# A matrix-square-root layer and a Fourier layer on 32x32 images: m and y side by side in one tile, the inverse transform's end in two matmuls, layer 0's statistics for two images at once, one scale for m and its transpose, and shorter roots

## The chip, the cores and the metric

The kernel runs on one core of one Trainium2 chip. The metric is the device time of one execution in microseconds (us); lower is better. The time before is the median of three runs.

## The reference

The input x holds 32 images of 32 channels of 128 x 128 numbers in fp32. Two layers follow each other, and each adds something to its input.

```
def _gn(v, G=16, eps=1e-5):          # mean and variance over 2 channels x 128 x 128
    return (g - m) / sqrt(s + eps)

def _L0_conv_ref(A):                 # for each of the 32*32 matrices of 128 x 128
    normA = sqrt(sum(A*A));  Y = A / normA;  Z = I
    for _ in range(5):
        T = 0.5 * (3*I - Z @ Y);  Y = Y @ T;  Z = T @ Z
    return Y * sqrt(normA)

def _L1_conv_ref(x, weights1, weights2):
    x_dht = fftn(x, axes=(2, 3)).real
    top = einsum('bixy,ioxy->boxy', x_dht[:, :, :32, :32], weights1)
    bot = einsum('bixy,ioxy->boxy', x_dht[:, :, -32:, :32], weights2)
    return ifftn(zeros with top and bot set in).real

x = x + _L0_conv_ref(_gn(x))
x = x + _L1_conv_ref(_gn(x), L1_conv_weights1, L1_conv_weights2)
```

Layer 0 is by far the larger part: 1024 matrices, each with a chain of products of 128 x 128 matrices.

## The kernel before

**Groups.** Four channels of one image make a group, so there are 256 groups. A group's four matrices are one tile of 128 partitions x 512 columns, and each PSUM bank holds one group's product. `products` (L304 to L308) is four TensorE matmuls, one for each matrix, into one bank; `transposed` (L310 to L314) is four TensorE transposes.

**The iteration.** The five steps of the reference are folded into two polynomials of fourth degree and a last linear one, in `newton` (L400) and `quartic` (L364). `quartic` forms v from the product mb m and from m (L367), then w, which is v transposed plus r, and q from the product v w plus a multiple of the identity (L394). After the first quartic ScalarE copies the product q m, scaled, out of PSUM as y (L404), then q y as m (L406), then m transposed as mb (L408). After the second quartic TensorE makes q m and q y, each as four matmuls with a 128-column moving operand and with q as the stationary one (L412). ScalarE writes the first as w in one instruction of 512 columns (L413) and the second as y, in four instructions of 128 columns, each with its own channel's scale (L416). VectorE turns the product w q into t (L418) and adds the product t y to the input, kept in xt (L420). Between such steps stands `yield from rest`, which is two yields.

**Near and far groups.** A "near" group's v is transposed by TensorE. A "far" group's v (images 1 to 18) is transposed in blocks by VectorE (L373), written to DRAM and read back in another order (L375, L383 or L386), and GpSimd adds r to it (L388), so TensorE has no transpose to do there.

**Order of the work.** A Python loop at the end writes all instructions out. It has nine lanes, each with one group under way, and goes round them; in each round a lane does one step of its group. A new group starts every 3 rounds (far) or 5 rounds (near). Side work is threaded in at fixed lanes of a round: the layer-0 statistics (`prep`), layer 1's forward transform (`settle`, `forward`, `summed`, `spectrum`), the products with the weights, and the inverse transform. Instructions inside `kept` stay in the order in which they were written on their queue; a planner may place the others differently. Every engine then works through its own queue in order.

**Layer 0's statistics.** `prep(b)` (L187) handles one image. It loads the image's transposed copy a second time, as eight tiles of 4 channels (L194, on ScalarE's DMA queue), and takes VectorE's `bn_stats` of each channel, 128 elements a partition (L202). `moments` (L162) sums means over the partitions with a matmul by a constant matrix (L172); a second such matmul sums the squares (L213). Then come some twenty small VectorE instructions, and two square roots by `root` (L150): ScalarE's Sqrt and one Newton step on VectorE in four instructions. The results are the scales and offsets with which `staged` (L333) normalizes a group: GpSimd writes m from xt (L348) and ScalarE writes mb, the matrix that is not transposed, in place (L359). Each has its own scale: sc and offm for m, scr and off for mb.

**Layer 1's statistics.** `summed` (L479) takes per-channel sums. One matmul with a stationary operand of 128 columns (q repeated four times over the columns, `b_qr`, L487) leaves the variance on all partitions (L492), and a second one with 32 columns gives the means (L495). `root` and a reciprocal give the inverse deviation (L502 to L504).

**The inverse transform.** `inverse` (L826) works on one image. Its end, for each half e of the channels, is three sets of four matmuls (L877). The four of a set use 32 rows of the array each and run side by side. The first set gives the cosine part (64 columns of each of four channels), the second the sine part (63 columns each), and the third one column of each channel, 4 in all, which goes to the place before the sine columns. ScalarE copies the second half of the columns out (L889), VectorE adds the first half to the image (L894).

**Room.** Tiles come from pools with a fixed number of buffers for each name (`rooms`, L259): y and m have four each, and two more while the pool for the early part stands. At the end `weights` (L743) loads the last group's weights into tiles of the layer-0 pools that are no longer needed, in the order of a list of names.

Of the kernel before, what the change touches and what calls it, by code (L numbers as in the profile page):

```python
# [48 lines left out]
EYE = 36 / 16  # L49
QS = EYE / QD  # L50
MS = -QA * QS
# [17 lines left out]
def conv_preact_kernel(  # L69
# [3 lines left out]
    xt_in: bass.AP,  # L73
    wk: bass.AP,
# [75 lines left out]
    def root(v, n, tag, f=1.0):  # L150

        s0 = small.tile([P, n], F32, tag=f"{tag}_s0", name=f"{tag}_s0")
        nc.scalar.activation(s0, v, AF.Sqrt, scale=1.0 / (f * f))
        q = small.tile([P, n], F32, tag=f"{tag}_q", name=f"{tag}_q")
        nc.vector.reciprocal(q, s0)
        nc.vector.tensor_mul(q, q, v)
        nc.vector.scalar_tensor_tensor(q, q, 1.0 / (f * f), s0, ALU.mult, ALU.add)
        s = small.tile([P, n], F32, tag=f"{tag}_s", name=f"{tag}_s", bufs=3)
        nc.vector.tensor_scalar_mul(s, q, 0.5 * f)
        return s  # L160

    def moments(st, tag):  # L162

        per = st.shape[1] // G
        f = st.rearrange("p (g c) (e t) -> p g (c e) t", c=per, t=3)
        ms = small.tile([P, G], F32, tag=f"{tag}_ms", name=f"{tag}_ms")
        nc.vector.tensor_reduce(ms, f[:, :, :, 1], AX.X, ALU.add)
        yield from pause  # L170
        pm = bank()[:, 0, 0:G]
        nc.tensor.matmul(pm, avg_mean, ms, start=True, stop=True)  # L172
        nm = small.tile([P, G], F32, tag=f"{tag}_nm", name=f"{tag}_nm", bufs=2)
        nc.vector.tensor_scalar_mul(nm, pm, 2 / per)
        d = small.tile([P, G, 2 * per], F32, tag=f"{tag}_d", name=f"{tag}_d")
        nc.vector.tensor_tensor(
            d, f[:, :, :, 1], nm[:, :, None].to_broadcast([P, G, 2 * per]), ALU.add
        )
        nc.vector.tensor_mul(d, d, d)
        nc.vector.scalar_tensor_tensor(d, d, 128.0 / per, f[:, :, :, 2], ALU.mult, ALU.add)  # L180
        return ms, nm, d
# [5 lines left out]
    def prep(b, made):  # L187

        st = small.tile([P, C, 6], F32, tag="a_st", name=f"a_st{b}", bufs=2)
        tiles = []  # L190

        def load(i):
            t = stp.tile([P, 4, P], F32, tag="xs", name=f"xs{b}_{i}")
            kept(nc.scalar.dma_start(out=t, in_=xt_in[b, :, 4 * i : 4 * i + 4, :]))  # L194
            tiles.append(t)

        for i in range(3):
            load(i)
        yield
        for i in range(C // 4):  # L200
            for c in range(4):
                nc.vector.bn_stats(st[:, 4 * i + c, :], tiles[i][:, c, :])  # L202
            yield
            if i + 3 < C // 4:
                load(i + 3)
        _, nm, d = yield from moments(st, "a")
        q = small.tile([P, C], F32, tag="a_qs", name=f"a_qs{b}")
        nc.vector.tensor_reduce(
            q, d.rearrange("p g (c e) -> p (g c) e", e=2), AX.X, ALU.add
        )  # L210
        yield from pause
        pq = bank()[:, 0, 0:C]
        nc.tensor.matmul(pq, avg_mean, q, start=True, stop=True)  # L213

        v = small.tile([P, C + G], F32, tag="a_v", name=f"a_v{b}")
        nc.vector.tensor_scalar_mul(v[:, 0:C], pq, -512 / (P * P))
        yield
        vg = small.tile([P, G], F32, tag="a_vg", name=f"a_vg{b}")
        nc.vector.tensor_reduce(
            vg, v[:, 0:C].rearrange("p (g c) -> p g c", c=2), AX.X, ALU.add  # L220
        )
        nc.vector.tensor_scalar(v[:, C:], vg, 0.5, EPS, ALU.mult, ALU.add)
        s = root(v, C + G, "a_r")
        iv = small.tile([P, C + G], F32, tag="a_inv", name=f"a_inv{b}")
        nc.vector.reciprocal(iv, s)
        yield

        sc = small.tile([P, C], F32, tag="a_sc", name=f"a_sc{b}", bufs=2)
        nc.vector.tensor_scalar_mul(sc, iv[:, 0:C], MS / P)
        n = small.tile([P, G, 2], F32, tag="a_n", name=f"a_n{b}")  # L230
        nc.vector.tensor_tensor(  # L231
            n,
            s[:, 0:C].rearrange("p (g c) -> p g c", c=2),
            iv[:, C:, None].to_broadcast([P, G, 2]),
            ALU.mult,
        )
        nn = small.tile([P, C], F32, tag="a_nn", name=f"a_nn{b}")
        nc.vector.tensor_scalar_mul(
            nn, n.rearrange("p g c -> p (g c)"), P * (1.5 / EYE) ** 2
        )  # L240
        sn = root(nn, C, "a_t")

        scr = small.tile([P, C], F32, tag="a_scr", name=f"a_scr{b}", bufs=2)
        nc.vector.tensor_scalar_mul(scr, sc, QR * QS / MS)
        off = small.tile([P, G, 2], F32, tag="a_off", name=f"a_off{b}", bufs=2)
        nc.vector.tensor_tensor(
            off,
            scr.rearrange("p (g c) -> p g c", c=2),
            nm[:, :, None].to_broadcast([P, G, 2]),
            ALU.mult,  # L250
        )
        off = off.rearrange("p g c -> p (g c)")
        offm = small.tile([P, C], F32, tag="a_offm", name=f"a_offm{b}", bufs=2)
        nc.vector.tensor_scalar_mul(offm, off, MS / (QR * QS))
        made[b] = (nm, sc, offm, sn, scr, off)
        yield


    rooms = dict(b=(4, 2), xt=(10, 4), x=(3, 2), r=(5, 2), v=(3, 3), w=(3, 2), q=(4, 2), y=(4, 2))  # L259
    rooms.update(m=(4, 2), mb=(2, 1), t=(3, 2), y4=(2, 2), turn=(0, 4))  # L260
    turns = dict.fromkeys(rooms, 0)

    def four(tag, more):
        n, m = rooms[tag]
        if more:
            turns[tag] += 1
            if turns[tag] % (n + m) >= n:
                return early.tile([P, 4, P], F32, tag=tag + "_early", name=tag, bufs=m)
        return sets.tile([P, 4, P], F32, tag=tag, name=tag, bufs=n)
# [63 lines left out]
    def staged(b, g, nm, sc, offm, sn, scr, off):  # L333
# [10 lines left out]
        for j in range(4):  # L344
# [12 lines left out]
            else:  # L357
                on_scalar(m[:, j, :], xt[:, j, :], offm, sc, c)
            on_scalar(mb[:, j, :], mb[:, j, :], off, scr, c)  # L359
# [4 lines left out]
    def quartic(m, mb, r, far, more, wide):  # L364


        v = plus(products(mb, m), -1 / (QA * QR * QS), m, "v", more)  # L367
# [26 lines left out]
        q = plus(products(v, w), 1 / (16 * QS * QS), eye, "q", more)  # L394
# [5 lines left out]
    def newton(g, sn, xt, m, mb, r, far, more):  # L400
# [3 lines left out]
        y = taken(products(q, m), "y", more, 1 / MS)  # L404
        yield from rest
        m = taken(products(q, y), "m", more, MS)  # L406
        yield from rest
        mb = taken(transposed(m), "mb", more, QR * QS / MS)  # L408
# [3 lines left out]
        pw, py = products(q, m), products(q, y)  # L412
        w, y = taken(pw, "t", more, 1 / MS), four("y4", more)  # L413
        for j in range(4):
            c = 4 * g + j
            nc.scalar.mul(y[:, j, :], py[:, j, :], sn[:, c : c + 1])  # L416
        yield from rest
        t = plus(products(w, q), -0.5 * EYE / 1.5, eye, "t", more)  # L418
# [60 lines left out]
    def summed(b, st):  # L479

        ms, _, d = yield from moments(st, "b")
        yield

        q = small.tile([P, G], F32, tag="b_qs", name=f"b_qs{b}")
        nc.vector.tensor_reduce(q, d, AX.X, ALU.add)
        qr = small.tile([P, 4, G, 2], F32, tag="b_qr", name=f"b_qr{b}")
        nc.vector.tensor_copy(qr, q[:, None, :, None].to_broadcast([P, 4, G, 2]))  # L487
        mr = small.tile([P, G, 2], F32, tag="b_mr", name=f"b_mr{b}")
        nc.vector.tensor_copy(mr, ms[:, :, None].to_broadcast([P, G, 2]))
        yield from pause  # L490
        pv = bank()[:, 0, :]
        nc.tensor.matmul(  # L492
            pv[:, 0:1], qr.rearrange("p l g c -> p (l g c)"), avg_v, start=True, stop=True
        )
        nc.tensor.matmul(  # L495
            pv[0:C, 1:2], mr.rearrange("p g c -> p (g c)"), avg_0, start=True, stop=True
        )
# [4 lines left out]
        s = root(v[:, 0:1], 1, "b_r", 256.0)  # L502
        r = small.tile([P, 1], F32, tag="b_inv", name=f"b_inv{b}")
        nc.vector.reciprocal(r, s)  # L504
# [238 lines left out]
    def weights():  # L743


        kinds = [("b", 2)] * 3 + [("x", 2), ("b", 4), ("x", 4), ("x", 10), ("y", 10), ("y", 10)]
        kinds += [("m", 11)] * 2 + [("r", 12)] * 4 + [("mb", 15)] * 2 + [("v", 15)] * 2
        kinds += [("w", 16)] * 2 + [("y", 16), ("m", 16), ("r", 17)] + [("q", 19)] * 3
        first = B * C // 4 - 10
        for half in range(4, 2 * KK):  # L750
            while True:
                if kinds and kinds[0][1] <= len(steps_of_last):
                    kind = kinds.pop(0)[0]
                    break
                if len(settled) > first and settled[first] < rounds - 4:
                    kind = "xt"
                    first += 1
                    break
                yield
            t = four(kind, False)  # L760
# [65 lines left out]
    def inverse(b):  # L826
# [37 lines left out]
        for e in range(2):  # L864
# [3 lines left out]
            py = [p.rearrange("p (s c h) -> p s c h", s=2, h=64) for p in py]  # L868
            cos, sin = (slice(T_IW.start + P * i, T_IW.start + P * i + P) for i in range(2))
            for s, table, h, g in (  # L870
                (0, cos, slice(0, 64), slice(0, 64)),
# [226 lines left out]
```

## Time and profile before

| what | value |
|---|---|
| median of 3 runs | 3066.74 us (3063.07 to 3076.99) |
| the profiled execution | 3080.12 us, its span 3078.2 us |
| TensorE busy | 2922.9 us, 95% of the span, 29504 matmul records |
| VectorE busy | 2374.3 us, 77%, 5242 instructions |
| GpSimd busy | 2001.8 us, 65% |
| ScalarE busy | 1634.7 us, 53% |
| mean granted TensorE clock | 0.982 |

The engines appear as PE (TensorE matmul), PEld (its weight load), DVE (VectorE), ACT (ScalarE), POOL (GpSimd) and SP (the DMA queue of SyncE). A matmul of fp32 data stands in the profile as two records, a transpose as one. A row of instructions gives line, engine, operation, tiles and shapes, the number of records, then busy time and the mean duration of one, and then the idle time of the engine just before them with what ended it. Matmuls overlap in the array, so the mean duration of one record is longer than the time from one start to the next. The program's line 307 is the matmul of `products`, line 313 that of `transposed`, and line 276 ScalarE's copy out of PSUM, so these lines stand for many places and are told apart by the names of their tiles.

### The profile page before, as it was taken

The numbers are of one execution on the slowest core, as the hardware profiler recorded it, in microseconds if no ns is written. First come the engines' busy times: TensorE is split into PE (matmuls) and PEld (weight loads), VectorE is DVE, ScalarE is ACT, GpSimd is POOL, SyncE is SP. The second block draws the span as 40 slices with busy tenths as digits, with TensorE's granted clock in tenths as the row PEclk, the third lists the DMA queues.
The fourth block names the chain that finished last, engine by engine and source line by source line (L and its number), as shares of the span: only waits on it lengthen the run. The fifth ranks groups of instructions, "written<-read, shape, count | busy, mean of one in ns | idle before, by whom it ended". The sixth has DMA issues, their size and how long they took to land.

```text
span 3078.2 us, 78788 instructions
## 1 busy us (share of the span) xinstructions
PE 2922.9 (95%) x29504; PEld 2801.7 (91%) x29504; DVE 2374.3 (77%) x5242; ACT 1634.7 (53%) x3961; POOL 2001.8 (65%) x2312
## 2 busy tenths in 40 slices
PE   6999999999999999999999999999999988999994
PEld 5899999999999999999999898998899988899894
DVE  6888888888888888888877656788778866878654
ACT  3565555655555655565544444554455544555552
POOL 4567677676776767767755435777686864767452
PEclk9999999999999999999999999999999999999995
DMA  3576676776766767666643566766676776665665
GB/s 128 168 216 214 207 214 210 219 216 206 219 210 213 216 209 220 202 208 206 211 133 100 174 206 210 240 227 225 226 231 216 256 254 201 222 213 200 209 214 206
DMA packets 475147, 636.74 MB, mean 207 GB/s; under 512 B 97040, under 2 KB 255248, under 8 KB 474768
## 3 DMA queue, kind: packets, MB, share of 16 engines
q1 hardware_dynamic: 361872, 425.88, 43.1%
q10 hardware_dynamic: 112896, 205.83, 21.6%
q8 instruction: 235, 3.85, 0.5%
q14 instruction: 144, 1.18, 0.1%
HBM read 402.42 MB, written 229.11 MB: 205 GB/s over the span
## 4 chain that ended last, share of the span: by engine, by line
PE 76%; DMA 10%; DVE 8%; ACT 1%; POOL 1%; issue 1%; SPq 1%; ACTq 0%; DVEq 0%; POOLq 0%
PE ps L307 62%; PE ps L313 6%; DMA xs<-in_xt 4%; PE ps L877 2%; PE ps L456 2%; DMA w<-turn 1%; PE ps L855 1%; DVE a_st L202 1%; PE ps L517 1%; PE ps L604 1%; DVE yt L894 1%; DMA diag<-in_wk 1%; DVE v L282 1%; PE ps L674 1%; DMA or<-od 1%
## 5 line engine op out<-in xcount | busy, mean ns | idle before, releaser
L307 PE MATMUL ps<-w,v 128*128 128x128 f32 x4096 | 550.8, 278 | 15.8 <-POOL w L388 8.1
L388 POOL TENSOR_TENSOR w<-w,r 128x512 f32<-128x512 f32 x288 | 366.7, 1276 | 305.9 <-DMA w<-turn 248.9
L341 ACT ACTIVATE b<-b,a_off,a_scr 128x128 f32<-128x128 f32 x1024 | 466.8, 489 | 170.5 <-issue 55.9
L307 PE MATMUL ps<-y,q 128*128 128x128 f32 x4096 | 532.1, 278 | 5.4 <-ACT d L889 2.1
L307 PEld LDWEIGHTS ps<-w,v 128*128 128x128 f32 x4096 | 500.5, 193 | 22.8 <-POOL w L388 9.6
L307 PEld LDWEIGHTS ps<-y,q 128*128 128x128 f32 x4096 | 495.3, 194 | 8.5 <-ACT d L889 2.3
L433 POOL TENSOR_TENSOR fold<-xt 128x256 f32<-128x256 f32 x512 | 364.2, 731 | 208.5 <-DVE xt L420 194.3
L282 DVE SCALAR_TENSOR_TENSOR q<-ps,eye 128x512 f32<-128x512 f32 x512 | 347.9, 680 | 147.7 <-PE ps L307 141.6
L823 POOL TENSOR_TENSOR yt<-yt,d 128x512 f32<-128x512 f32 x248 | 311.1, 1281 | 153.7 <-ACT d L889 131.0
L301 POOL TENSOR_TENSOR r<-mb,eye 128x512 f32<-128x512 f32 x112 | 142.8, 1275 | 302.2 <-ACT mb L276 295.3
L348 POOL TENSOR_SCALAR x<-xt,a_nm,a_sc 128x128 f32<-128x128 f32 x736 | 324.9, 453 | 20.1 <-DVE a_n L231 20.1
L416 ACT ACTIVATE y<-ps,a_t_s 128x128 f32<-128x128 f32 x1024 | 292.1, 368 | 60.6 <-PE ps L307 60.4
L202 DVE BATCH_NORM_STATS2 a_st<-xs 128x6 f32<-128x128 f32 x1024 | 228.7, 278 | 93.5 <-DMA xs<-in_xt 93.2
L307 PE MATMUL ps<-m,q 128*128 128x128 f32 x2048 | 277.5, 279 | 13.4 <-DVE q L282 9.3
L307 PE MATMUL ps<-m,mb 128*128 128x128 f32 x2048 | 276.1, 278 | 6.0 <-ACT d L889 4.3
L307 PE MATMUL ps<-x,b 128*128 128x128 f32 x2048 | 274.5, 277 | 6.8 <-POOL x L348 5.6
L307 PE MATMUL ps<-x,q 128*128 128x128 f32 x2048 | 276.1, 278 | 4.5 <-DVE q L282 2.9
L276 ACT ACTIVATE t<-ps 128x512 f32<-128x512 f32 x256 | 152.3, 595 | 240.5 <-PE ps L307 227.3
L307 PE MATMUL ps<-y,t 128*128 128x128 f32 x2048 | 275.7, 278 | 3.0 <-DVE t L282 2.0
L307 PE MATMUL ps<-q,t 128*128 128x128 f32 x2048 | 274.9, 278 | 0.0
L307 PEld LDWEIGHTS ps<-m,q 128*128 128x128 f32 x2048 | 252.1, 194 | 16.6 <-DVE q L282 10.4
L276 ACT ACTIVATE y<-ps 128x512 f32<-128x512 f32 x256 | 152.5, 596 | 215.8 <-PE ps L307 202.7
(145 smaller groups left out, 5779.7 us busy)
## 6 DMA issues: line engine op xcount, KB each, us to landing
turn<-turn SPq DMA_DIRECT2D x288, 256.0 KB
b<-in_x ACTq DMA_DIRECT2D x256, 256.0 KB
xt<-in_xt ACTq DMA_DIRECT2D x256, 256.0 KB
xs<-in_xt ACTq DMA_DIRECT2D x256, 256.0 KB
mid<-xt SPq DMA_DIRECT2D x256, 256.0 KB
yt<-mid SPq DMA_DIRECT2D x128, 512.0 KB
out<-yt SPq DMA_DIRECT2D x120, 512.0 KB
w<-turn SPq DMA_DIRECT2D x144, 256.0 KB
```

What stands on the lines that cost most here:

```text
L202: nc.vector.bn_stats(st[:, 4 * i + c, :], tiles[i][:, c, :])
L276: nc.scalar.mul(t, ps, f)
L282: nc.vector.scalar_tensor_tensor(s, ps, f, t, ALU.mult, ALU.add)
L301: nc.gpsimd.tensor_tensor(r, mb, eye, ALU.add)
L307: nc.tensor.matmul(ps[:, j, :], lhsT[:, j], rhs[:, j], start=True, stop=True)
L313: nc.tensor.transpose(ps[:, j, :], t[:, j, :], ident)
L341: nc.scalar.activation(t, x, AF.Identity, bias=offset[:, c], scale=scale[:, c])
L348: nc.gpsimd.tensor_scalar(m[:, j, :], xt[:, j, :], nm[:, c // 2 : c // 2 + 1], sc[:, c : c + 1], ALU.add, ALU.mult,)
L388: nc.gpsimd.tensor_tensor(w, w, r, ALU.add)
L416: nc.scalar.mul(y[:, j, :], py[:, j, :], sn[:, c : c + 1])
L433: nc.gpsimd.tensor_tensor(f[:, :, 64 * half : 64 * half + 64], xt[:, :, 0:64], xt[:, :, 64:128], op)
L823: engine.tensor_tensor(yh, yh, d, op)
```

## The change

Seven things change.

1. y and m lie in one tile `my` of [128, 4, 2, 128], y first. After the second quartic one matmul per matrix multiplies q with both, a moving operand of 256 columns, into two banks of two matrices each. ScalarE copies w out in two instructions of 256 columns, one for each bank.
2. m and mb have the same scale MS = 1/QR. The constants EYE and QF take up the factors; the second scale and offset (scr, offm) go, and mb is copied without a factor. In the v step the operands change places: m times a factor, plus the product in PSUM.
3. `prep` works on a list of images: image 0, image 1, then pairs. A pair's statistics start when group 4 of the image two before is staged. Small tiles are twice as wide.
4. The statistics are read from a new input, `in_xs`, a copy of x on which two channels of a normalization group are interleaved element by element. One `bn_stats` of 256 elements then serves two channels, because it keeps the even and the odd elements apart.
5. `root` has no scale factor.
6. In `summed` the two copies become one; the 128-column stationary operand becomes 32 columns used by four matmuls that write 32 partitions each. The inverse deviation comes from 1/Sqrt and one Newton step for the reciprocal root.
7. The inverse transform's end has two sets of matmuls, 65 and 63 columns of each channel, in place of three. `weights` takes a `my` tile as two halves.

```
-    def prep(b, made):
+    def prep(bs, made):
...
-            t = stp.tile([P, 4, P], F32, tag="xs", name=f"xs{b}_{i}")
-            kept(nc.scalar.dma_start(out=t, in_=xt_in[b, :, 4 * i : 4 * i + 4, :]))
+            t = stp.tile([P, 2, 2 * P], F32, tag="xs", name=f"xs{b}_{i}")
+            src = xs_in[b, :, 2 * i : 2 * i + 2].rearrange("p g h c -> p g (h c)")
+            kept(nc.scalar.dma_start(out=t, in_=src))
...
-            for c in range(4):
-                nc.vector.bn_stats(st[:, 4 * i + c, :], tiles[i][:, c, :])
+            for j in range(2):
+                nc.vector.bn_stats(st[:, 2 * k + j, :], tiles[k][:, j, :])
...
-        v = plus(products(mb, m), -1 / (QA * QR * QS), m, "v", more)
+        v = plus(m, -QA * MS, products(mb, m), "v", more)
...
-        y = taken(products(q, m), "y", more, 1 / MS)
+        my = four("my", more)
+        y = my[:, :, 0, :]
+        nc.scalar.mul(y, products(q, m), 1 / (MS * QF))
         yield from rest
-        m = taken(products(q, y), "m", more, MS)
+        m = my[:, :, 1, :]
+        nc.scalar.mul(m, products(q, y), MS / QF)
         yield from rest
-        mb = taken(transposed(m), "mb", more, QR * QS / MS)
+        mb = taken(transposed(m), "mb", more)
...
-        pw, py = products(q, m), products(q, y)
-        w, y = taken(pw, "t", more, 1 / MS), four("y4", more)
+        both = [bank().rearrange("p (j k) x -> p j k x", k=2) for _ in range(2)]
+        for j in range(4):
+            nc.tensor.matmul(both[j // 2][:, j % 2], q[:, j], my[:, j], start=True, stop=True)
+        w, y = four("t", more), four("y4", more)
+        for h in range(2):
+            nc.scalar.mul(w[:, 2 * h : 2 * h + 2, :], both[h][:, :, 1, :], 1 / (MS * QF))
         for j in range(4):
             c = 4 * g + j
-            nc.scalar.mul(y[:, j, :], py[:, j, :], sn[:, c : c + 1])
+            nc.scalar.mul(y[:, j, :], both[j // 2][:, j % 2, 0, :], sn[:, c : c + 1])
...
-        qr = small.tile([P, 4, G, 2], F32, tag="b_qr", name=f"b_qr{b}")
-        nc.vector.tensor_copy(qr, q[:, None, :, None].to_broadcast([P, 4, G, 2]))
-        mr = small.tile([P, G, 2], F32, tag="b_mr", name=f"b_mr{b}")
-        nc.vector.tensor_copy(mr, ms[:, :, None].to_broadcast([P, G, 2]))
+        wide = small.tile([P, 2, G, 2], F32, tag="b_wide", name=f"b_wide{b}")
+        nc.vector.tensor_copy(wide, mq[:, :, :, None].to_broadcast([P, 2, G, 2]))
...
-        nc.tensor.matmul(
-            pv[:, 0:1], qr.rearrange("p l g c -> p (l g c)"), avg_v, start=True, stop=True
-        )
+        for i in range(4):
+            rows = slice(C * i, C * i + C)
+            nc.tensor.matmul(pv[rows, 0:1], wide[:, 1, :], avg_v, start=True, stop=True)
...
-            for s, table, h, g in (
-                (0, cos, slice(0, 64), slice(0, 64)),
-                (1, sin, slice(1, 64), slice(65, 128)),
-                (1, cos, slice(0, 1), slice(64, 65)),
-            ):
+            for table, h in ((cos, slice(0, 65)), (sin, slice(65, 128))):
...
-    preps.append(prep(0, made))
+    preps.append(prep([0], made))
+    coming = [((0, 0), [1])] + [((b - 2, 4), [b, b + 1]) for b in range(2, B, 2)]
```

## The prediction

> **What bounds the kernel now.** I read four views: the page's busy shares, the stretches of time, TensorE's timeline at full pace, and the groups of instructions by shape with the waits.
>
> First the page, then the stretches between the start-up and the end (columns: length, then busy time of PE, PEld, DVE, ACT and POOL, granted clock, DMA share, GB/s).
>
> ```profile
> PE 2922.9 (95%) x29504; PEld 2801.7 (91%) x29504; DVE 2374.3 (77%) x5242; ACT 1634.7 (53%) x3961; POOL 2001.8 (65%) x2312
> ```
> ```profile
> 200.00:1540.00 1340.00, 1329.54 (x11985) 1291.66 (x11984) 1128.07 (x2527) 790.80 (x1946) 961.38 (x1062) 1.00 0.69 211
> 1540.00:2960.00 1420.00, 1351.17 (x15234) 1281.54 (x15233) 1037.40 (x2233) 709.44 (x1694) 886.96 (x1072) 0.99 0.64 206
> ```
>
> TensorE is idle for 10 of 1340 us in the far part and for 69 of 1420 us in the near part. No other engine passes 84%. But busy matmuls overlap, so the timeline has to say whether TensorE runs at its pace (columns: start, length, engine, instruction, count).
>
> ```profile
> 1500.66 1.06 PE L307 MATMUL ps<-q,t 128*128 128x128 f32 x8
> 1501.55 1.06 PE L307 MATMUL ps<-w,v 128*128 128x128 f32 x8
> 1502.45 1.06 PE L307 MATMUL ps<-x,b 128*128 128x128 f32 x8
> 1503.34 1.06 PE L307 MATMUL ps<-m,q 128*128 128x128 f32 x8
> 1504.23 1.06 PE L307 MATMUL ps<-y,q 128*128 128x128 f32 x8
> ...
> 1505.66 0.61 PE L456 MATMUL ps<-fold,tab 128*32 128x504 f32 x1
> ...
> 1506.10 0.59 PE L456 MATMUL ps<-fold,tab 128*32 128x504 f32 x1
> ```
>
> Eight records follow each other every 0.893 us: 0.1116 us for one record of 128 columns, and no gaps. The last two lines are two passes of about 512 columns: 0.44 us apart, four column groups running side by side. So the pace is that of the moving columns. The path that sets the end is TensorE's own queue, and only what shortens that queue or its idle time counts.
>
> ```profile
> L307 PE MATMUL ps<-q,t 128*128 128x128 f32 x2048 | 274.9, 278 | 0.0
> L877 PE MATMUL ps<-gt,tab 32*128 32x256 f32 x512 | 48.1, 443 | 3.7 <-ACT gt L861 3.7
> L877 PE MATMUL ps<-gt,tab 32*128 32x252 f32 x512 | 40.8, 387 | 0.0
> L877 PE MATMUL ps<-gt,tab 32*128 32x4 f32 x512 | 19.8, 211 | 0.0
> ```
> ```profile
> PE ps L172 <- DVE a_ms L169: 15.9, 1, 15.9
> PE ps L307 <- DVE q L282: 12.3, 9, 4.2
> PE ps L307 <- DVE w L282: 11.2, 7, 3.4
> ```
>
> The waits of TensorE are few: on VectorE 61 us over all its rows, 16 of them the very first matmul. The product w q never waited (the first of the four rows above).
>
> **The change part by part.** The sum is made against the profiled execution (3080 us, span 3078); the median is 13 us lower, and I carry the difference over unchanged.
>
> *q times (m, y) in one matmul.* Before: 256 groups x 8 matmuls x 2 records = 4096 records of 128 columns. After: 2048 of 256 columns. The columns are the same; only the fixed part of a pass is saved. No full-array pass of 256 columns is in this trace, so I bound it. A straight line through 0.1116 us (128) and 0.44 us (504 to 512) gives 0.218 us; the pair before takes 0.2232. The gain is 5 ns x 2048 = 11 us. Ends: the line with the fixed part gone altogether (0.44 x 256 / 512 = 0.22, or 0.216 if the 512 pass takes 0.43) gives at most 15 us; a pass that costs two of 128 gives 0. Here the Trainium skill ("TensorE: Matmul & The Clock Gate", Back-to-back issue gap) says more: in a stream of weight loads and matmuls the spacing is set by both, about 81 ns at 128 columns and 131 ns at 512. A straight line between gives 98 ns at 256, so 2 x 81 - 98 = 64 ns a pass pair, and x 2048 an estimate of 131 us. The timeline contradicts it for this kernel: 128 to 512 columns go from 0.112 to 0.44 us, nearly in proportion, so weight loads are already hidden. I take the row: 11 us.
>
> *w from two banks.* w and y now wait for all of the wider stream: the second half of w is ready at 8 x 0.218 + 0.376 = 2.12 us after its start (0.376 us is the 128x256 copy of L889), where before it was 0.893 + 0.595 = 1.49 us. That is 0.63 us later, and ScalarE is busy for 2 x 0.376 - 0.595 = 0.16 us more a group, 40 us in all (53% to 54%). The cover is the two yields before w q: a near group starts every 5 rounds and takes roughly 11 us of TensorE (44 matmuls of 0.223 us and more), so a round is about 2.2 us, two rounds 4.4. Behind the late w on ScalarE's queue stand the four y copies and the next lanes' copies, for which v, mb and r wait. Price taken: 0. Without the cover: 0.63 us for each group that is exposed.
>
> *The inverse's end.* 64 sets lose two passes of 4 columns (19.8 us busy, 512 records); two passes grow by 4 columns (0.86 ns a column from 0.44/512, 7 ns a set). The 4-column group is the last of its set, and its length is largely the switch back to full-array matmuls, which remains. I take half of the 19.8, less 0.5: 9 us. Ends 2 and 19. A rule speaks against this edit: the skill ("SBUF — State Buffer", Door 1) says that a non-contiguous PSUM access significantly slows matmuls, and runs of 65 columns with a step of 128 are such. If that doubled two passes of 0.22 us in 64 sets, it would cost 28 us. But the 252-column row already writes runs of 63 with a step of 64, and its mean is 387 ns where the contiguous 256 columns have 443. I price it at 0.
>
> *Layer 0's statistics.* TensorE: 64 small matmuls become 34. One took 0.145 us (0.15 us at 118.06 in the timeline, 0.14 at 113.38): 64 x 0.145 - 34 x 0.155 = 4 us saved. VectorE: `bn_stats` 228.7 us becomes that of the b_st row, 512 of the same shape, 207.8: -21. The 24 small a_ instructions an image sum to 262 us (341 ns each); after, 21 x 17 lists x 370 ns, an estimate for the doubled width, = 132: -130. The loads are as many and as large, 256 KB each on ScalarE's queue; in a pair, 16 of them are spread over about 48 rounds as before, and a pair's 26 or so steps have 36 to 60 rounds, so none is late. A pair's chain of small instructions blocks VectorE for about as long as an image's did, but half as often.
>
> *Shorter roots, one scale.* b_ instructions: one copy less (12 us), the root's four or five tiny ones (54 us) become four without the slow SBUF products (L156: 810 ns each): -35 in all. The swapped operands of v I price like the w row and the t y row, 680 ns whichever side is in PSUM: 0. TensorE pays in `summed`: four matmuls with 32-column stationaries in place of one with 128. Before, the pair of rows took 0.36 us (261.63 to 261.99). Four column groups side by side as at L468 (0.13 us for four records) make it the same; one after the other at the 0.15 us of L495 makes 0.75, 12 us over 32 images. I take 3.
>
> *What VectorE's relief is worth.* 21 + 130 + 35 = 186 us off 2374, 71% busy. In the far part nothing of it is on the path: TensorE has 10 us of idle there. In the near part TensorE's idle on VectorE is about 45 us over all rows; at 8% less load I take 5. The start saves some five small instructions of 0.2 us on the first image's chain and a shorter `bn_stats` behind the last load: 2. The last loads of weights into `my` halves come at most a round later: 0.
>
> The sum: -11 - 9 - 4 + 3 - 5 - 2 = -28 us. From 3066.7 that is **3039 us**, 0.9% less.
>
> **The rivals.**
>
> *A: the wide matmul and the inverse save next to nothing.* The wide pass costs two (0.223) and the switch stays: -28 + 11 + 7 = -10, 3057 us. For it: the proportional pace of the timeline. Against: the small fixed part that 0.1116 shows over 0.44/4 = 0.110.
>
> *B: the stalls go too.* In 1540 to 2960 us TensorE idles 69 us, and in several slices after 1540 the granted clock is below 1 behind such idles. If a lighter VectorE took a third of about 90 us, 30 more go: 3009 us. For it: the q and w waits above. Against: the other idles come from ScalarE, DMAs and group changes, which the change leaves.
>
> *C: slower.* The second half of w comes too late for w q, in the near part, where ScalarE also copies for the inverse transform. Price 0.63 us a group, from 28 / 0.63 = 44 exposed groups on it eats the gain; all of the 100 near groups after 1540 us give 3039 + 63 = 3102 us. Against: the w q row has 0.0 us of idle over 2048 records.
>
> **How the numbers follow.** My forecast 0.54, A 0.20, B 0.19, C 0.07. The likeliest one's own range is 3022 to 3054: the ends of the wide pass, the inverse and `summed`. The 8-in-10 range runs from B to just past A: 3006 to 3062; C and a deeper B are left out. A change of 0.5%, 15 us, is about what a measurement can tell from none, so faster means below 3051. Of my forecast nine tenths and all of B are below it, with a little of A: 0.71. Most of A and the rest of the forecast: 0.22. C: 0.07.
>
> **What would show it.** The timeline of the changed kernel should have eight records of 256 columns in 1.74 us (1.73 to 1.79); the inverse's set about 1.05 us where it was 1.19; TensorE 27456 + 192 - 512 - 60 = some 27,080 records; VectorE about 2190 us busy, ScalarE 1670. The far stretch should shrink by about 10 us, for its 144 groups and its statistics. I am wrong if w q shows idle on ScalarE's t, if the wide pass leaves 0.218 by more than 5 ns, or if TensorE's idle in the near part moves by more than 15 us either way: the planner may place the products anew, and that I can't cost from the trace.

## The result

The changed kernel takes 3041.4 us (median of four, 3032.1 to 3042.9) where the kernel before, on the same chip, takes 3069.2 us. The ratio is 0.9898 with a 95% interval of 0.9878 to 0.9918: about 1.0% faster. A second series gave 0.9902 (0.9879 to 0.9924). The forecast was 3039 us. The profiled execution took 3040.4 us, its span 3038.6 us.

Times of different series drift by a few us, so below every kernel is compared by its ratio to the kernel before on the same chip; 0.001 is 3 us.

First the page's busy line, then the two stretches (length, busy PE, PEld, DVE, ACT, POOL, granted clock, DMA share, GB/s).

```profile
PE 2893.8 (95%) x27076; PEld 2684.5 (88%) x27076; DVE 2219.3 (73%) x4255; ACT 1636.0 (54%) x4187; POOL 1997.6 (66%) x2312
```
```profile
200.00:1540.00 1340.00, 1326.39 (x11066) 1253.72 (x11064) 1072.19 (x2045) 797.29 (x2071) 967.00 (x1070) 1.00 0.69 215
1540.00:2960.00 1420.00, 1360.80 (x14211) 1240.97 (x14209) 968.45 (x1846) 718.77 (x1815) 897.10 (x1083) 0.99 0.64 209
```

TensorE runs 27076 records, as counted in the prediction. VectorE is 155 us less busy, ScalarE as busy as before. TensorE is still nearly gapless in the far stretch, and in the near one it idles 59 us where it idled 69. Its timeline (start, length, instruction, count) shows the price of the wide pass and of the two small edits on its queue:

```profile
1500.05 1.06 PE L305 MATMUL ps<-x,b 128*128 128x128 f32 x8
1500.94 1.89 PE L415 MATMUL ps<-my,q 128*128 128x256 f32 x8
1502.67 1.05 PE L305 MATMUL ps<-my,q 128*128 128x128 f32 x8
```
```profile
1696.64 0.24 PE L498 MATMUL ps<-avg_v,b_wide 128*32 128x1 f32 x8
1696.72 0.20 PE L499 MATMUL ps<-avg,b_wide 128*32 128x1 f32 x2
1696.86 0.66 PE L311 MATMUL ps<-ident,my 128*128 128x128 f32 x4
...
1888.34 1.15 PE L883 MATMUL ps<-gt,tab 32*128 32x260 f32 x16
1889.41 1.16 PE L305 MATMUL ps<-my,mb 128*128 128x128 f32 x8
```

In the kernel before, the sums of layer 1 and an inverse set looked like this:

```profile
261.63 0.28 PE L492 MATMUL ps<-avg_v,b_qr 128*128 128x1 f32 x2
261.84 0.22 PE L495 MATMUL ps<-avg,b_mr 128*32 128x1 f32 x2
261.99 1.16 PE L307 MATMUL ps<-q,t 128*128 128x128 f32 x8
...
1900.26 1.26 PE L877 MATMUL ps<-gt,tab 32*128 32x256 f32 x24
1901.45 0.66 PE L313 MATMUL ps<-ident,v 128*128 128x128 f32 x4
```

Eight passes of 256 columns go by in 1.73 us, 0.216 each, where two of 128 took 0.223. The sums of layer 1 take 0.22 us (1696.64 to 1696.86) where they took 0.36. An inverse set takes 1.07 us (1888.34 to 1889.41) where it took 1.19.

Then the groups by shape that the prediction watched, and TensorE's longest waits:

```profile
L415 PE MATMUL ps<-my,q 128*128 128x256 f32 x2048 | 493.3, 384 | 7.8 <-DVE q L280 5.2 <-ACT d L895 2.4
L305 PE MATMUL ps<-q,t 128*128 128x128 f32 x2048 | 274.5, 277 | 3.2 <-ACT d L895 1.6 <-ACT t L418 0.9 <-DVE yt L900 0.7
...
L883 PE MATMUL ps<-gt,tab 32*128 32x260 f32 x512 | 50.3, 444 | 4.7 <-ACT gt L871 4.7
L883 PE MATMUL ps<-gt,tab 32*128 32x252 f32 x512 | 42.4, 387 | 0.0
```
```profile
PE ps L170 <- DVE a_ms L167: 14.5, 1, 14.5
PE ps L305 <- ACT d L895: 13.6, 7, 5.2
PE ps L305 <- POOL w L386: 12.1, 14, 4.2
```

The product w q waits 0.9 us in all for its later w (the profile calls it t, after its tile). TensorE's waits on VectorE over all rows are 42 us where they were 61, those on q and w 13 where they were 23; the waits on ScalarE's d and GpSimd's w grew (16 us for 11, 12 for 8).

**Where the time went.** From the records' starts I split TensorE's time into its queue's own pace (0.1116 us for each record of 128 columns, 0.109 for a transpose, 0.216 for 256 columns, the small sets as long as they are without a wait) and the gaps on top.

| us | before | after | difference |
|---|---|---|---|
| products of 128 and 256 columns | 2285.5 | 2270.7 | -14.8 |
| inverse's end (L877 / L883) | 80.1 | 73.6 | -6.5 |
| layer 0's statistics | 10.5 | 6.2 | -4.3 |
| layer 1's statistics | 17.4 | 12.2 | -5.2 |
| everything else | 433.4 | 431.9 | -1.5 |
| queue, sum | 2826.9 | 2794.6 | -32.3 |
| gaps | 221.9 | 216.4 | -5.5 |

The gaps hold idle time and records that ran slower than that pace. In stretches of 3 to 7 us the granted clock is 0.50 (the windows 2514.2:2520.9 of before and 2574.5:2581.2 of after show two); between 200 and 2960 us they sum to 48 us before, 34 after and 48 in a second profile of the changed kernel. In that second profile the gaps were 222.6. So the queue became 32 us shorter and the gaps stayed what they were, within what two profiles of one kernel differ by. The eighth group's last product starts 3.3 us sooner (135.7 us for 139.0), the 144th 13.6 us sooner, so the far part gave 10.3 us; the rest lies behind it. The profile of before was of an execution 11 us above its median, so the profiles differ by 39.6 us and the medians by 28. The queue's 32 us are as much as the medians and ratios show (28 to 31 us): nothing of the gain is left for smaller gaps.

### The profile page after: what moved, and what is told of

It reads as the page before. It is cut to its first block, busy times and chain, and to the rows that moved or that the text cites. A ratio compares the mean times of both kernels' runs of the same rounds, so it can differ in the third digit from the quotient of the medians.

```text
span 3038.6 us, 73447 instructions
## 1 busy us (share of the span) xinstructions
PE 2893.8 (95%) x27076; PEld 2684.5 (88%) x27076; DVE 2219.3 (73%) x4255; ACT 1636.0 (54%) x4187; POOL 1997.6 (66%) x2312
## 4 chain that ended last, share of the span: by engine, by line
PE 75%; DMA 10%; DVE 9%; POOL 2%; issue 2%; ACT 2%; SPq 1%; ACTq 0%; DVEq 0%; POOLq 0%
PE ps L305 49%; PE ps L415 12%; PE ps L311 6%; DMA w<-turn 3%; DMA xs<-in_xs 3%; PE ps L461 2%; PE ps L883 2%; DMA or<-od 1%; PE ps L612 1%; DVE yt L900 1%; PE ps L865 1%; DVE a_st L206 1%; DVE v L280 1%; DVE turn L371 1%; PE ps L682 1%
## 5 line engine op out<-in xcount | busy, mean ns | idle before, releaser
L339 ACT ACTIVATE b<-b,a_off,a_sc 128x128 f32<-128x128 f32 x1024 | 467.3, 491 | 177.5 <-issue 45.6
L415 PE MATMUL ps<-my,q 128*128 128x256 f32 x2048 | 493.3, 384 | 7.8 <-DVE q L280 5.2
L415 PEld LDWEIGHTS ps<-my,q 128*128 128x128 f32 x2048 | 373.2, 192 | 53.3 <-DVE q L280 4.7
L418 ACT ACTIVATE t<-ps 128x256 f32<-128x256 f32 x512 | 192.6, 384 | 237.3 <-PE ps L415 229.4
L421 ACT ACTIVATE y<-ps,a_t_s 128x128 f32<-128x128 f32 x1024 | 312.4, 372 | 0.0
L305 PE MATMUL ps<-my,q 128*128 128x128 f32 x2048 | 276.7, 278 | 6.0 <-ACT d L895 3.9
L305 PE MATMUL ps<-my,mb 128*128 128x128 f32 x2048 | 275.9, 278 | 6.5 <-ACT d L895 5.2
L206 DVE BATCH_NORM_STATS2 a_st<-xs 128x6 f32<-128x256 f32 x512 | 195.4, 412 | 112.6 <-DMA xs<-in_xs 112.0
L305 PEld LDWEIGHTS ps<-my,q 128*128 128x128 f32 x2048 | 260.8, 193 | 17.4 <-ACT d L895 4.5
L404 ACT ACTIVATE my<-ps 128x512 f32<-128x512 f32 x256 | 152.7, 596 | 229.2 <-PE ps L305 211.1
```

The lines of the kernel that those rows point to most:

```text
L206: nc.vector.bn_stats(st[:, 2 * k + j, :], tiles[k][:, j, :])
L305: nc.tensor.matmul(ps[:, j, :], lhsT[:, j], rhs[:, j], start=True, stop=True)
L339: nc.scalar.activation(t, x, AF.Identity, bias=offset[:, c], scale=scale[:, c])
L415: nc.tensor.matmul(both[j // 2][:, j % 2], q[:, j], my[:, j], start=True, stop=True)
L418: nc.scalar.mul(w[:, 2 * h : 2 * h + 2, :], both[h][:, :, 1, :], 1 / (MS * QF))
L421: nc.scalar.mul(y[:, j, :], both[j // 2][:, j % 2, 0, :], sn[:, c : c + 1])
```

## The experiments

The theory, "columns": TensorE's queue sets the time, the wide pass saves only its fixed part, and VectorE's relief is worth little. The rivals: A, the wide pass saves nothing; B, VectorE's relief is what counts; C, the later w costs.

### The changed kernel again

> The changed kernel once more, so that its neighbours are compared with it on the same chip. Expected near 3041 us, ratio 0.989 to 0.991 to the kernel before.

3045.3 us, ratio 0.9902 (0.9879 to 0.9924). The kernels below are compared with 0.990, 30 us below the kernel before.

### The wide matmul undone, and alone

```
-        both = [bank().rearrange("p (j k) x -> p j k x", k=2) for _ in range(2)]
...
+        pw, py = products(q, my[:, :, 1, :]), products(q, my[:, :, 0, :])
+        w, y = four("t", more), four("y4", more)
+        nc.scalar.mul(w, pw, 1 / (MS * QF))
```

> The changed kernel with the wide matmul undone: q m and q y as two sets of four matmuls of 128 columns, w copied in one instruction; my stays one tile. Theory 'columns' (the queue of TensorE, only the fixed part of a pass is saved): the changed kernel's trace has the 256-column pass at 0.2155 us, so 2048 x (0.2232 - 0.2155) = 16 us come back, 3057 us against 3041. Rival A (the wide pass saves nothing, the gain lies in the other parts): 3041 to 3044. The skill's stream figures (81 and 131 ns): 130 us come back.

3065.8 us, ratio 0.9970 (0.9957 to 0.9983): 21 us come back, give or take 8. The other direction, this part alone on the kernel before (the `my` tile and the wide matmul as in the diff above):

> The kernel before with the first part alone: m and y in one tile and the wide matmul, all else as it was. Theory 'columns': 16 us faster than the kernel before, about 3053 (ratio 0.995). Rival A: as before, 3069. If the parts need each other (the wide matmul pays only with a lighter VectorE): as before or slower.

3051.6 us, ratio 0.9936 (0.9918 to 0.9955): 20 us faster. Both directions agree, and with 16 us within their intervals. Rival A is out, and so is the 131 us that the prediction estimated from the Trainium skill's stream figures ("TensorE: Matmul & The Clock Gate", Back-to-back issue gap): in these traces a record takes 0.112 us at 128 columns and 0.216 at 256. The part pays without the others, so it does not need a lighter VectorE.

### The inverse's end in three sets again

```
-            for table, h in ((cos, slice(0, 65)), (sin, slice(65, 128))):
+            for s, table, h, g in (
+                (0, cos, slice(0, 64), slice(0, 64)),
+                (1, sin, slice(1, 64), slice(65, 128)),
+                (1, cos, slice(0, 1), slice(64, 65)),
+            ):
```

> The changed kernel with the inverse's end in three sets of matmuls again. Theory 'columns' (a set takes 0.11 us less with two, as the traces show it): 64 x 0.11 = 7 us slower than the changed kernel, 3048 us. If long runs with an odd step slowed the matmuls or the copies that read them, or the switch were all of the third set's length: the same as the changed kernel or faster, 3041 or less.

3049.7 us, ratio 0.9923 (0.9900 to 0.9945): 6 us slower than the changed kernel by the middle values, where 7 were expected, but the interval reaches from 3 us faster to 16 slower. In its profile the inverse's matmuls take 80.2 us of the queue, against 73.6; that is the firmer number.

### More and less on VectorE

Two instructions with both operands in SBUF after each loaded tile:

```
+            for j in range(2):
+                all4 = tiles[k].rearrange("p g x -> p (g x)")
+                nc.vector.tensor_tensor(all4, all4, all4, ALU.add)
```

> The changed kernel with two more VectorE instructions of 512 columns after each loaded tile of layer 0's statistics, 512 in all, about 0.68 us each: some 340 us more on VectorE, nearly twice what the change took off (155 us by the two traces); nothing reads their results. Theory 'columns' (VectorE's relief is worth about 5 us): 5 to 12 us slower than the changed kernel, 3046 to 3053. Rival B (VectorE's load sets TensorE's stalls): at 155 us for 20 to 30 us, 45 to 65 us slower, 3085 to 3105.

3289.8 us, ratio 1.0696 (1.0673 to 1.0718): 244 us slower, far beyond what either theory gave. The stretches, the new instruction and TensorE's longest waits in that kernel:

```profile
200.00:1540.00 1340.00, 1242.07 (x10037) 1162.80 (x10036) 1170.84 (x2091) 724.93 (x1886) 933.58 (x965) 0.98 0.63 194
```
```profile
L209 DVE TENSOR_TENSOR xs<-xs 128x512 f32<-128x512 f32 x512 | 454.5, 892 | 0.2
```
```profile
PE ps L418 <- DVE q L283: 39.0, 23, 4.1
PE ps L308 <- DVE t L283: 34.9, 27, 3.6
PE ps L308 <- DVE q L283: 27.1, 23, 2.9
```

VectorE reaches 87% of the far stretch, TensorE waits for its q and t, and idles 98 us there where it idled 14. Each new instruction took 892 ns, not the 680 of those with one operand in PSUM, and GpSimd's got longer too (its x from 450 to 499 ns). So this dose had two things in it, VectorE's load and longer instructions on GpSimd, and doesn't tell them apart.

The opposite: one pair of statistics in eight is made, its result copied.

```
-            for j in range(2):
-                nc.vector.bn_stats(st[:, 2 * k + j, :], tiles[k][:, j, :])
+            if k % 8 == 0:
+                for j in range(2):
+                    nc.vector.bn_stats(st[:, 2 * k + j, :], tiles[k][:, j, :])
+                nc.vector.tensor_copy(
+                    st[:, 2 * k + 2 : 2 * k + 16, :].rearrange("p (i j) t -> p i j t", j=2),
+                    st[:, None, 2 * k : 2 * k + 2, :].to_broadcast([P, 7, 2, 6]),
+                )
```

> The changed kernel with seven of eight pairs of statistics instructions of layer 0 left out, each image's first result copied in their place (so the scales are wrong): some 170 us less on VectorE, which the change had already relieved by 155 us. Everything else, loads too, stays. Theory 'columns': 0 to 6 us faster, 3035 to 3041. Rival B: another 20 to 30 us faster, 3011 to 3021.

3015.8 us, ratio 0.9803 (0.9782 to 0.9823): 30 us faster. By the profiles 9 of them come before the eighth group (126.4 us for 135.7), as TensorE's first matmul starts at 8.7 us and not at 14.5; 3 to 7 come in the far part and 16 to 22 in the near part, against the two profiles of the changed kernel. That speaks for B more than for the theory.

A dose with one operand in SBUF, 157 us by its instructions' durations:

```
+            for j in range(1 + (k + 1) % 2):
+                waste = small.tile([P, 6], F32, tag="waste", name=f"waste{first_b}_{k}_{j}", bufs=2)
+                nc.vector.bn_stats(waste, tiles[k][:, j, :])
```

> The changed kernel with 384 more statistics instructions of 256 elements on VectorE, one or two after each loaded tile of layer 0's statistics, results unread: 384 x 0.41 = 157 us, the load that the change took off VectorE, put back evenly and without a second operand in SBUF. The theory after the first eight runs (VectorE's relief is worth 10 to 15 us between the load before and the load after): 10 to 15 us slower than the changed kernel, 3051 to 3056, nearly all as gaps in TensorE's queue. The theory of the prediction (5 us): 3043 to 3047. If the added instructions of the earlier double dose slowed the kernel mainly through GpSimd (their two operands in SBUF): no more than 5 us here either.

3075.6 us, ratio 1.0009 (0.9996 to 1.0021): 33 us slower than the changed kernel, twice the new theory and all that the change had gained.

```profile
PE 2904.6 (95%) x27076; PEld 2693.9 (88%) x27076; DVE 2330.9 (76%) x4639; ACT 1636.6 (53%) x4187; POOL 1995.6 (65%) x2312
```
```profile
200.00:1540.00 1340.00, 1327.27 (x11087) 1256.78 (x11086) 1133.41 (x2258) 799.59 (x2076) 964.91 (x1070) 1.00 0.70 215
1540.00:2960.00 1420.00, 1347.10 (x14010) 1228.15 (x14010) 992.97 (x1949) 710.50 (x1793) 887.49 (x1074) 0.98 0.63 204
```

VectorE is busy 112 us more, since instructions overlap, and short of the kernel before's 2374. The far part hardly changes (1387.1 us from the eighth group to the 144th, 1386.5 and 1382.7 in the two profiles of the changed kernel), even with VectorE at 85%: there the cover is real. Before the eighth group 9 us are lost, 2 to 3 of them before the first matmul: three quarters as many statistics again stand in the first image's chain. From the 144th group to the 248th it takes 1376 us, against 1359 and 1365. So the near part and the start pay for these instructions, the far part hardly. What they cost is not the price of what the change took off, as the last kernel of the next section shows.

### The statistics for two images: undone and alone

```
-    coming = [((0, 0), [1])] + [((b - 2, 4), [b, b + 1]) for b in range(2, B, 2)]
+    coming = [((b - 1, 0), [b]) for b in range(1, B)]
```

> The changed kernel with layer 0's statistics made for one image at a time, started when the image before is staged; the interleaved input and the 256-element statistics stay. That brings back 15 x 21 small VectorE instructions (about 100 us) in their bursts, and 30 small matmuls. Theory 'columns': 15 x 0.3 = 4 us on TensorE and 0 to 4 us of stalls, 3045 to 3049. Rival B (relief, and bursts above all): 15 to 20 us slower, 3056 to 3061.

3057.5 us, ratio 0.9946 (0.9927 to 0.9965): 14 us slower than the changed kernel, give or take 9; the interval holds rival B's 15 to 20 and the upper part of the theory's 4 to 8. Next, parts 2 to 5 of the change alone: the changed kernel, its `my` tile kept, with the wide matmul, the inverse and layer 1's sums as they were:

> The statistics for two images, the interleaved input, one scale and the shorter root alone: the wide matmul, the inverse's two sets and the new sums of layer 1 are undone. VectorE keeps some 130 us of its relief; TensorE's queue keeps 4 us. Theory after the first eight runs (relief is worth 10 to 15 us): 13 to 18 us faster than the kernel before, about 3056. The theory of the prediction: 4 + 5 = 9 us, about 3062. If the parts give nothing alone because gaps elsewhere take it back: as before, 3070.

3070.5 us, ratio 1.0002 (0.9984 to 1.0020): no gain, give or take 6, though the trace has layer 0's matmuls at 6.2 us of the queue for 10.5 and VectorE at 1076 us of the far stretch for 1128. The remaining case, everything but the statistics of layer 0, which stay exactly as they were (parts 1, 6 and 7 on the kernel before, root left long for layer 0):

> The kernel before with the wide matmul, the inverse's two sets and the new sums of layer 1, but with layer 0's statistics exactly as they were (one image at a time, 128 elements an instruction, two scales, the long root). If the parts add up, as the wide matmul alone (20 us) and the pairs alone (0 us) suggest: 29 us faster than before, about 3042, the same as the changed kernel, and the slowdown of the kernel with one image at a time was its own order. If the pairs pay once TensorE's queue is shorter, as that kernel suggests: 15 to 20 us faster than before, about 3054, and the rest of the gain is the pairs'. By the prediction's terms: 9 to 11 us slower than the changed kernel, 3051.

3053.0 us, ratio 0.9930 (0.9905 to 0.9954): 9 us slower than the changed kernel, give or take 10. So parts 2 to 5 give 0 (give or take 6) alone and 9 (give or take 10) beside the others; the intervals overlap, so these two runs leave open whether the parts add up.

This kernel also corrects the reading of the dose of statistics above. Its busy line:

```profile
PE 2904.5 (95%) x27136; PEld 2695.9 (88%) x27136; DVE 2331.2 (76%) x5178; ACT 1639.0 (54%) x4217; POOL 1996.2 (65%) x2312
```

VectorE is as busy here as with the dose (2331.2 and 2330.9 us), and TensorE has 4 us more in its queue, yet this kernel is 24 us faster (0.9930 against 1.0009), give or take 8. So the 33 us of the dose are not the price of VectorE's busy time as such. Which instructions are added, where they stand, or how the planner then orders the rest may set it; no run separates these.

### A later w

```
-        for h in range(2):
-            nc.scalar.mul(w[:, 2 * h : 2 * h + 2, :], both[h][:, :, 1, :], 1 / (MS * QF))
         for j in range(4):
             c = 4 * g + j
-            nc.scalar.mul(y[:, j, :], both[j // 2][:, j % 2, 0, :], sn[:, c : c + 1])
+            kept(
+                nc.scalar.mul(y[:, j, :], both[j // 2][:, j % 2, 0, :], sn[:, c : c + 1])
+            )
+        for h in range(2):
+            kept(
+                nc.scalar.mul(w[:, 2 * h : 2 * h + 2, :], both[h][:, :, 1, :], 1 / (MS * QF))
+            )
```

> The changed kernel with w copied out after the four copies of y, so that w comes 0.7 to 1.5 us later than now. Theory 'columns' (two rounds cover w): 0 to 5 us slower, 3041 to 3046, and the product w q shows idle of some us on ScalarE's t at most. Rival C (the late w has little room): 0.7 us for a good part of the 256 groups, 50 us and more, above 3090.

3057.5 us, ratio 0.9954 (0.9941 to 0.9966): 16 us slower, between the two.

```profile
L305 PE MATMUL ps<-q,t 128*128 128x128 f32 x2048 | 275.2, 278 | 8.2 <-ACT t L424 4.4 <-ACT d L899 3.1 <-DVE yt L904 0.7
```

The product itself waits only 5 us longer (8.2 us for 3.2), so its gaps are not where most of the loss is. The edit also binds the order of six copies among ScalarE's other ones, and what that did was not separated. So rival C's price for a late w is out, but where the 16 us go stays open.

### The two sets in the other order

```
-            for table, h in ((cos, slice(0, 65)), (sin, slice(65, 128))):
+            for table, h in ((sin, slice(65, 128)), (cos, slice(0, 65))):
```

> The changed kernel with the two sets of the inverse's end in the other order, sine first. The work is the same on every engine; ScalarE's copies of the sine columns, which come first on its queue, can begin half a microsecond earlier. It shows what an edit without any work in it does to the gaps in TensorE's queue. Theory 'gaps depend on the planner's order by some 10 us': between 3031 and 3051. Theory 'gaps follow the load': 3038 to 3042.

3041.5 us, ratio 0.9901 (0.9881 to 0.9922): the same as the changed kernel. Its gaps are 219.1 us, between the two profiles of that kernel. An edit without work in it moved nothing here. The value lies in the range of both theories, so it doesn't decide between them; and an edit that changes the order little doesn't exclude that a larger one moves the time more. How much of the differences above is the planner's new order stays open.

## Why the prediction was right

The forecast was 28 us less; the medians differ by 28, the ratios by 30. The path was right: TensorE's queue sets the time, and shortening it is what the gain came from. The agreement of the sum is in part luck. Step by step:

- **q times (m, y)**: right in mechanism, and small, as forecast. But the working has a slip: a straight line through 0.1116 us (128 columns) and 0.44 us (512) gives 0.221 us at 256, not 0.218, and so 4 us, not 11; 0.218 needs 0.43 us at 512. The pass took 0.216, the forecast's far end, and the term 15 us. Undone and alone the time moved by 21 and 20 us, which may hold a few us beyond the pass.
- **w from two banks**: priced at 0, and w q waits 0.9 us for t, so nothing of the 0.63 us a group is seen. ScalarE's copies of w take 40 us more, as forecast (192.6 us for 152.3), but its busy time, in which overlapping copies count once, stayed at 1636 us where 1670 was forecast.
- **The inverse's end**: 9 us taken, 6.5 measured in the queue. The half was right and the whole was wrong: the 4-column group's 19.8 us are busy time, and by the starts of its records it takes 0.228 us a set, 14.6 us in 64 sets. The last record of a set is followed by the next full-array record after 0.300 us where the steady pass has 0.193, so 0.107 of the 0.228 us moved there and stayed. Runs of 65 columns with a step of 128 cost nothing: 0.219 us for 260 columns in the four-tile pass that has no switch in it, against 0.216 for 256. The slowdown of the Trainium skill ("SBUF — State Buffer", Door 1) did not show.
- **Layer 0's statistics on TensorE**: 4 us, measured 4.3.
- **Layer 1's sums**: mis-sized, with the wrong sign. The prediction added 3 us; the queue lost 5.2. The four 32-column matmuls start 7 ns apart and run side by side, and one load of 32 columns lasts 109 ns where that of 128 lasted 195. Even the lower bound, side by side as at L468, had them no shorter than before.
- **VectorE's work**: 186 us less forecast, 155 measured. The doubled small instructions of layer 0 took 430 ns and not 370, so that their sum fell by 108 us and not by 130; those of layer 1 fell by 57 and not by 35. The rest is overlap: the durations of all instructions fell by 237 us, but many overlapped their neighbours, and busy time counts those stretches once.
- **What that relief is worth**: 5 us behind the start and 2 at the start. At the start 1.4 to 3.3 us were gained; behind it the two profiles show no change of gaps beyond their spread. With parts 2 to 5 undone the time is 9 us longer, give or take 10, where the prediction's terms for them make 11 (4, 5 and 2). That is agreement within a wide interval, not proof. The reason given for the near part, that TensorE's idle on VectorE is 45 us and the relief a small share of it, is not a safe one: these waits fell by 17 us, not 5, and others took their place; and the dose of 112 us brought back 16 us of TensorE's waits on VectorE (57 us for 41 and 42) but cost 33.
- **The rivals**: B's further 30 us, 3009, did not come, and C's 3102 and A's 3057 lie outside the interval of the measured ratio.

So errors of both signs met. In TensorE's queue 21 us were forecast and 32 measured: the wide pass and the sums of layer 1 gave 12 us more, the inverse 2.5 less. In the gaps and at the start 7 us were forecast, and beside the queue's 32 the medians leave nothing for them. Why the changed kernel's gaps are no smaller than before, though the dose on VectorE stretched the time from TensorE's first matmul to its last by 23 to 30 us, stays open. A shorter queue on TensorE leaves less time for the same work of the others, which would fit, but no run separates that from the order in which the planner puts the instructions.

## What to carry to other kernels

Where one engine runs at its pace, count its queue: the gain of an edit is the number of its records by the time from start to start, not by their duration or busy time (the 4-column group above: 14.6 us by starts, 19.8 busy). Two matmuls with one stationary operand, made one, save only the fixed part of a pass when the weight loads are hidden already (7 ns of 223 here, 2048 times). And the load of an engine that is not the bound can't be priced safely by the bound engine's waits on it, nor by other instructions put in its place: two kernels with the same VectorE busy time differed by 24 us. Undo the part itself, often enough that the interval is narrower than the price.

## What was not expected of the hardware

Instructions of VectorE with both operands in SBUF took 892 ns at 512 columns beside a GpSimd that is busy 64% of the time, where those with one operand in PSUM take 680; GpSimd's own became 2 to 11% longer in that run. The kernel before has eight such VectorE instructions already (L823, `yt` plus `d`), and they take 1306 ns each. `bn_stats` of 256 elements takes 0.41 us where two of 128 take 0.56 (by busy time the gain is smaller, 195 us for 229 in all), and with two channels interleaved one instruction gives the statistics of both, as the changed kernel uses it.
